# In every fourth slot, TensorE's update of W stands one pair of experts later

## The chip, the cores and the metric

The kernel runs on one core of one Trainium2 chip. The metric is the device time of one execution in microseconds (us), lower being better. Before the change three runs took 1006.75, 1006.24 and 1005.19 us; the median is 1006.24 us. PE is TensorE's matmul stream and PEld its weight loads, DVE is VectorE, ACT ScalarE, POOL GpSimd, SP the engine whose queue issues the DMAs.

## The reference, cut to what matters

The input x has 8 batches of 1024 time steps with 256 features, in float32. It is normalised (layer norm), and two things are computed from the result:

```python
xn = _layernorm(x, axis=-1)
# s: a linear layer learned online, one gradient step of W per time step
v = xn @ Wkv[d:].T + bkv[d:]
def step(W, inp):
    xt, vt = inp
    y = xt @ W.T
    gW = (2.0 / (b * d)) * ((y - vt).T @ xt)
    return (W - eta * gW, y)
# g: silu of a mixture of 16 linear experts, the gates being
#    the top 6 of a softmax over router logits, made to sum to one
out = sum over e of (xn @ expert_w[e]) * gate[:, e:e + 1]
x + s * silu(out)
```

## The kernel before, in words

**Tiles and slots.** The tokens go in 64 tiles of 128 rows: 16 time steps of all 8 batches. The main loop (lines 653 to 661) goes through the tiles i, and for each through eight pairs of experts. The stretch of the loop that belongs to tile i is called slot i here; a place in it is written (slot, pair) or as one number, 8 * slot + pair. At each place the function `experts` (line 530) does its pair: six matmuls (line 241) of 128x128 by 128x512 make `h`, one PSUM bank of 512 columns, 256 for each expert. There are three such banks (line 85), so a pair can only be started when the bank of the pair three places earlier has been read by both of its readers.

**Who reads h.** The even expert is multiplied by its gate and added to a running sum on DVE (`mix`, line 558). The odd one is multiplied by its gate on ACT (`part`, line 547) and added on POOL (line 550); this holds for experts 1 to 11. Experts 13 and 15 go to DVE like the even ones (line 47). So pair 3 is read by `mix_6` on DVE and `part_7` on ACT, and so on.

**The recurrence over W.** W^T lives in one PSUM bank, `wt_ps`. A tile goes through three steps, one after the other, and each needs the one before:

- `errors_1` (line 488): six matmuls of X with the current W (`pe`), then DVE and ACT make `p`, `p_hi`, `p_lo`.
- `errors_2` (line 505): three matmuls with the solved matrix U; then ACT makes `step_hi` (line 510) and DVE makes `step_lo` (line 512), and DVE also `hy` (line 516).
- `update` (line 518): six matmuls into `wt_ps`, of 128x128 by 128x256: hi by hi, lo by hi, hi by lo for each half of the features. The third and the sixth read `step_lo`. Then `new_state` (line 159) makes `wt_hi` on ACT (line 142) and `wt_lo` on DVE (line 143), which `errors_1` of the next tile reads.

**What sets the order.** TensorE and SP keep the order in which the code issues work (line 639). A table of events says what comes ahead of which pair. From tile 7 on, `errors_1`, `errors_2` and `update` of tile i come ahead of pairs 0, 3 and 5 of slot i; tiles 0 to 6 have places of their own (line 607), among them slot 6, where the update comes ahead of pair 7. The other engines are put in an order by a scheduler when the kernel is built; on the chip each engine then takes its instructions strictly in that order.

**Gates and U come by groups.** Gates, and the triangular solve for U, are made for four tiles at a time. The work of a group of tiles first to first + 3 lies ahead of it: each tile is projected five slots early, at pair 1 (`project_x`, line 583), and the last tile of a group also sets off `gates` (line 348), a row of about twenty small DVE operations. That happens in slots 6, 10, 14 and so on to 58. In the same slot DVE makes the first matrices of the solve (`q`, line 407), and TensorE does the first step of it, `q_ps` (`step_q`, line 395), ahead of pair 6. Because events at one place are done in the order in which they were put, and the recurrence is put first, an update at pair 6 would come ahead of `q_ps`.

Of the kernel before, what the change touches and what calls it, by code (L numbers as in the profile page):

```python
"""Layer norm, then an online-learned linear layer (one gradient step of W per time step) gated by
the silu of a top-6-of-16 mixture of linear experts, with a residual.

Tokens go in tiles of 128 rows: 16 time steps of all 8 batches, time-major. Within a tile the
recurrence is solved exactly: with A = c * X X^T restricted to strictly earlier time steps and
c = eta * 2 / (B * D), the errors of all steps are E = T (X W^T - V), T = (I + A)^-1, where W is the
weight before the tile, and W^T is then lowered by c * X^T E. The state W^T accumulates in one PSUM
bank.

U = T^T is built for a few tiles at a time from diagonal blocks of 32 rows, by Horner's rule  # L10
(I - C (I - C (I - C)), C = A^T), which merge into blocks of 64 and then 128 rows:
U_ab = -U_a C_ab U_b.

TensorE and the DMA queue keep the order given below; the other engines are scheduled around them.
All but the first tiles are transposed without TensorE: in blocks of 32 by VectorE, and the blocks
change places on their way through DRAM.

The large products split each float32 operand exactly into two float32r parts, x = hi + lo, and add
up hi*hi + hi*lo + lo*hi in float32; what is left out is below float32's own rounding.
"""  # L20

# [1 line left out]

# [11 lines left out]
PSUM = bass.MemoryType.PSUM  # L35
# [5 lines left out]
EPS = 1e-10  # L41
ABSENT = -3.0e38
TAKEN = 3.0e38
GROUP = 4
# [6 lines left out]
def ttt_moe_kernel(  # L51
# [13 lines left out]
    B, S, D = x.shape  # L65
# [10 lines left out]
    state = ctx.enter_context(tc.tile_pool(name="state", bufs=2))  # L76
# [3 lines left out]
    work = ctx.enter_context(tc.tile_pool(name="work", bufs=2))  # L80
# [10 lines left out]
    where = []  # L91
# [19 lines left out]
    def misc(name):  # L111
        return ps_misc.tile([P, 512], F32, tag="misc", name=name)

# [1 line left out]
    raws = {}  # L115

    def fetch_expert(e):
# [19 lines left out]
    make_identity(nc, ident)  # L137
    neg_half = const.tile([P, 1], F32)
    nc.gpsimd.memset(neg_half, -0.5)
    # transposed weights: W0^T the first state, [Wv^T | router^T] one moving operand  # L140
    def split(hi, lo, src, engine=None):
        nc.scalar.copy(hi, src)  # L142
        (engine or nc.vector).tensor_sub(lo, src, hi.bitcast(F32))  # L143
# [37 lines left out]
    def at(b, size=Q):  # L181
        return slice(b * size, (b + 1) * size)

# [1 line left out]
    class Prepared:  # L185
        pass

    tiles = {}

    def layernorm(i):  # L190
        q = tiles[i] = Prepared()
        xt = x_tile(i)
        st = small.tile([P, nc.vector.BN_STATS_DIM], F32, tag="st", name=f"st_{i}")
        nc.vector.bn_stats(st, xt)  # L194
        mv = small.tile([P, nc.vector.BN_AGGR_DIM], F32, tag="mv", name=f"mv_{i}")
        nc.vector.bn_aggr(mv, st)  # L196
        ve = small.tile([P, 1], F32, tag="ve", name=f"ve_{i}")
        nc.gpsimd.tensor_scalar_add(ve, mv[:, 1:2], LN_EPS)  # L198
        rstd = small.tile([P, 1], F32, tag="rstd", name=f"rstd_{i}")
        nc.gpsimd.tensor_tensor(rstd, ve, neg_half, ALU.pow)  # L200
        q.xn = work.tile([P, D], F32, tag="xn", name=f"xn_{i}", bufs=3)
        nc.vector.tensor_scalar(q.xn, xt, mv[:, 0:1], rstd, ALU.subtract, ALU.mult)  # L202
        if i < BY_PE:
            return
        q.xT = work.tile([P, KD * P], F32, tag="xT", name=f"xT_{i}", bufs=3)
        # blocks of 32 are transposed in place, and change places by way of DRAM
        xr = work.tile([P, D], F32, tag="xr", name=f"xr_{i}")
        nc.vector.transpose(
            xr.rearrange("p (c k t) -> p k c t", c=NQ, k=KD),
            q.xn.rearrange("p (k c t) -> p k c t", c=NQ, k=KD),  # L210
        )
        bounce = dram.tile([NQ, Q, NQ, KD * Q], F32, tag="bounce", name=f"bounce_{i}")
        nc.sync.dma_start(out=bounce.rearrange("b d c f -> (b d) (c f)"), in_=xr)
        for c in range(NQ):
            nc.sync.dma_start(
                out=q.xT[at(c), :].rearrange("p (b f) -> p b f", b=NQ),
                in_=bounce[:, :, c, :].rearrange("b d f -> d b f"),
            )
# [15 lines left out]
        split(q.xn_hi, q.xn_lo, q.xn, nc.gpsimd)  # L234

    def accumulate(o, hi, lo, rhs_hi, rhs_lo, first=True, **kw):
        # the terms with the moving low part come last: it is ready last
        terms = [t for a, b, r in zip(hi, lo, rhs_hi) for t in ((a, r), (b, r))]
        terms += zip(hi, rhs_lo)
        for m, (a, b) in enumerate(terms):  # L240
            nc.tensor.matmul(  # L241
                o, lhsT=a, rhs=b, start=first and m == 0, stop=(m == len(terms) - 1), **kw
            )

    def project(i, g, j):
        q = tiles[i]
        # X X^T = H H^T + H L^T + (H L^T)^T
        gram = misc(f"gram_{i}")
        for k in range(KD):
            nc.tensor.matmul(  # L250
                gram[:, : 2 * P], lhsT=q.xT_hi[:, k, :],
                rhs=q.xT_two[:, k, :, :].rearrange("p n t -> p (n t)"),
                start=(k == 0), stop=(k == KD - 1), skip_group_check=True,
            )
        q.gram, q.cross = gram, work.tile([P, P], F32R, tag="cross", name=f"cross_{i}")
        nc.scalar.copy(q.cross, gram[:, P : 2 * P])
        vr = misc(f"vr_{i}")
        accumulate(
            vr[:, :NVR],
            [q.xT_hi[:, k, :] for k in range(KD)], [q.xT_lo[:, k, :] for k in range(KD)],  # L260
            [w_vr[0][:, k, :] for k in range(KD)], [w_vr[1][:, k, :] for k in range(KD)],
        )
        nc.vector.tensor_add(g.lg[:, j, :NE], vr[:, D:NVR], bias[:, D:])  # L263
        q.vr = vr
# [11 lines left out]
        nc.vector.tensor_add(xx, q.gram[:, :P], q.cross.bitcast(F32))  # L276
        nc.vector.tensor_mul(g.a[:, j, :, :], xx.unsqueeze(1).broadcast_to([P, 2, P]), masks)

# [1 line left out]
    layernorm(0)  # L280
    transpose_w()
    ident_r = const.tile([P, P], F32R)
# [2 lines left out]
    for b in range(NQ):  # L285
# [3 lines left out]
    half_b = const.tile([P, D], F32)  # L289
    nc.scalar.mul(half_b, bias[:, :D], 0.5)  # L290

    # -c at strictly earlier time steps, in A's place and in A^T's
    ones = const.tile([P, P], F32)
    nc.gpsimd.memset(ones, 1.0)
    keep = const.tile([P, 2, P], F32)
    nc.gpsimd.affine_select(
        out=keep[:, 0, :], in_=ones, compare_op=ALU.is_ge, fill=0.0, base=-B,
# [3 lines left out]
        out=keep[:, 1, :], in_=ones, compare_op=ALU.is_gt, fill=0.0, base=0,  # L301
# [2 lines left out]
    masks = const.tile([P, 2, P], F32)  # L304
    nc.vector.tensor_scalar_mul(masks, keep, neg_c)

    # U and the first half of T by blocks: what is never written stays zero
    u_full, t_half = [], []
    for n in range(2):
        u = const.tile([P, GROUP, P], F32, tag=f"u_{n}", name=f"u_{n}")  # L310
# [8 lines left out]
    def open_group(n, first, count):  # L319
# [14 lines left out]
        for name, t in vars(stores[m]).items():  # L334
            if name in ("t", "z2"):
                setattr(g, name, t)
            else:
                setattr(g, name, t[:, j : j + count])
        # odd tiles keep the first half of T, and what comes of it, in the upper partitions
        g.halves = []  # L340
        for odd in range(2):
            js = [n for n in range(count) if (j + n) % 2 == odd]
# [5 lines left out]
    def gates(g):  # L348
# [5 lines left out]
        def narrow(name):  # L354
            return group.tile([P, GROUP], F32, tag=name, name=f"{name}_{n}", bufs=4)[:, :c]

        # the six largest logits, the first of equal ones, are marked; two absent values fill up to eight
        lg, top, d, ex = g.lg, wide("top", 8), wide("d"), wide("ex")
        marked, chosen, gate = wide("marked", NE + 2), wide("chosen"), wide("gate", bufs=4)
        for j in range(c):  # L360
# [12 lines left out]
            chosen, marked[:, :, :NE], TAKEN, ex, op0=ALU.is_equal, op1=ALU.mult  # L373
        )
        nc.vector.tensor_reduce(s_top, chosen, AX.X, ALU.add)
        # gates p / (sum p + EPS) with p = ex / s_all, then divided by max(their sum, EPS)
        nc.vector.scalar_tensor_tensor(den, s_all, EPS, s_top, op0=ALU.mult, op1=ALU.add)
        nc.vector.reciprocal(r_den, den)
        nc.vector.tensor_mul(total, s_top, r_den)
# [7 lines left out]
            q.u_hi, q.u_lo = g.u_hi[:, j, :], g.u_lo[:, j, :]  # L387

    def step_q(g, name, rhs, out):
        """I - C rhs for the diagonal blocks."""  # L390
        c = g.count
        ps = solving(f"{name}_ps_{g.n}")
        for j in range(c):
            for b in range(P // Q):
                nc.tensor.matmul(  # L395
                    ps[at(b), j * Q : (j + 1) * Q], lhsT=g.a[at(b), j, 0, at(b)],
                    rhs=rhs[at(b), j, :], start=True, stop=True, skip_group_check=True,
                )
        nc.vector.tensor_add(
            out, ps[:, : c * Q].rearrange("p (j q) -> p j q", q=Q),  # L400
            ident_q.unsqueeze(1).broadcast_to([P, c, Q]),
        )
# [58 lines left out]
    H = P // 2  # L461
# [22 lines left out]

    solve = [solve_1, solve_2, solve_3, solve_4, solve_5, solve_6]

# [1 line left out]
    def errors_1(i):  # L488
        q = tiles[i]
        q.pe = ps_rec.tile([P, 2 * D], F32, tag="pe", name=f"pe_{i}")  # L490
# [70 lines left out]
                q.mix[j] = new  # L561

    def finish(i):
        # x + y silu(m) = x + (y / 2) m (1 + tanh(m / 2))
        q = tiles[i]
        xt = x_tile(i)
        m = work.tile([P, D], F32, tag="m", name=f"m_{i}")
# [9 lines left out]
            out=out[:, i * TS : (i + 1) * TS, :].rearrange("b t d -> t b d"), in_=o  # L577
        )

# [1 line left out]
    opened = {}  # L581

    def project_x(i):
# [13 lines left out]
    def solve_x(n, m):  # L597
        solve[m](opened[n])

    # what comes before each (tile, pair of experts)  # L600
    events = {}

    def put(slot, pair, what, *args):
        events.setdefault((slot, pair), []).append((what, args))

    # the first tiles have a schedule of their own: (slot, pair) as 8 * slot + pair
    chain = {
        0: (3, 9, 10), 1: (13, 16, 18), 2: (21, 23, 25), 3: (27, 29, 31), 4: (33, 38, 40),
        5: (42, 45, 47), 6: (49, 51, 55),
    }  # L610
    for i in range(NT):
        spots = chain.get(i, (8 * i, 8 * i + 3, 8 * i + 5))
        for what, spot in zip((errors_1, errors_2, update), spots):
            if what is not update or i + 1 < NT:
                put(spot // 8, spot % 8, what, i)
        if i + 1 < NT:
            put(i + 1, 1, finish, i)
# [75 lines left out]
```

## Time and profile before

| What | Value |
|---|---|
| Median of three runs | 1006.24 us (1005.19 to 1006.75) |
| Profiled execution: span from first to last instruction | 1004.7 us |
| Matmuls of the experts (`h`), 3072 | 789.3 us, mean 402 ns each (they overlap) |
| Matmuls of the update (`wt_ps`), 126 of each of three kinds | 35.6, 35.6 and 37.0 us |
| Share of the span in which DVE, ACT, POOL are busy | 77%, 43%, 44% |
| Mean granted TensorE clock | 0.992 of full speed |

The profiled execution has only its span; what lies around the first and the last instruction is in the times of the three runs, which are 0.5 to 2.1 us above the span. In the groups of instructions a row names the line, the engine, the operation, what is written and read, and how often, then busy time, mean duration of one, and the idle time just ahead of them with what ended it. In a timeline a row has the start and the length in us, both from the span's start. A line such as L241 or L142 can be that of a helper that many steps call; the name of the tile then tells the steps apart. A matmul's row includes its filling and draining, so rows of matmuls overlap: what a matmul costs the stream is the distance from its start to the next start.

### The profile page before, as it was taken

To read this page: it belongs to the slowest core of one execution; us is meant where nothing else is said; L and a number is where in the kernel's file an instruction comes from. 1 tells how busy PE (TensorE), PEld (TensorE's weight loads), DVE (VectorE), ACT (ScalarE), POOL (GpSimd) and SP (SyncE) were. 2 spreads that over 40 slices of the span, in tenths; PEclk is the share of its full clock that TensorE was granted. 3 is DMA by queue.
4 is the path that set the end of the run, shared out by engine and by line. 5 is a ranking of instruction groups with operands and counts; after the bars stand their busy time and mean duration, and the time that the engine had idled before them with its cause. 6 is when DMAs were issued, how large, how long until landed. Compare 5 with 4: busy or idle time off the path is not lost.

```text
span 1004.7 us, 19617 instructions
## 1 busy us (share of the span) xinstructions
PE 977.6 (97%) x6672; PEld 799.9 (80%) x6672; DVE 770.0 (77%) x2225; ACT 436.5 (43%) x1174; POOL 440.8 (44%) x677
## 2 busy tenths in 40 slices
PE   5899999999999999999999999999999999999997
PEld 4677888878888887888878888887888878888785
DVE  7888797777878777787777878778787777867665
ACT  5454444344443534435344443534435344443432
POOL 6544344444344344444444344344444444344333
PEclk8899999999999999999999999999999999999999
DMA  7021111111111111111111111011111111100000
GB/s 231 17 53 49 39 27 43 37 27 43 39 27 42 28 37 43 38 27 44 38 28 43 38 28 43 24 42 43 36 29 43 38 28 43 35 25 11 12 11 11
DMA packets 67092, 38.65 MB, mean 38 GB/s; under 512 B 38176, under 2 KB 66992, under 8 KB 66992
## 3 DMA queue, kind: packets, MB, share of 16 engines
q1 hardware_dynamic: 66992, 37.41, 13.6%
q8 instruction: 52, 0.85, 0.3%
q14 instruction: 48, 0.39, 0.1%
HBM read 21.13 MB, written 16.25 MB: 37 GB/s over the span
## 4 chain that ended last, share of the span: by engine, by line
PE 77%; DVE 14%; issue 2%; POOL 2%; DMA 2%; ACT 2%; SPq 1%; POOLq 0%; DVEq 0%; ACTq 0%
PE h L241 59%; PE pe L241 6%; PE wt_ps L241 4%; PE vr L241 3%; DVE q L407 3%; DVE mix L558 2%; DMA x<-in_L_attn_x_dram 1%; PE gram L250 1%; DVE marked L366 1%; POOL mix L550 1%; DVE st L194 1%; ACT part L547 1%; DVE o L574 1%; DVE d L362 1%; PE uq_ps L395 1%
## 5 line engine op out<-in xcount | busy, mean ns | idle before, releaser
L241 PE MATMUL h<-we,xT_two 128*128 128x512 f32 x3072 | 789.3, 402 | 4.5 <-DVE mix L558 2.5
L241 PEld LDWEIGHTS h<-we,xT_two 128*128 128x128 f32 x3072 | 554.5, 189 | 120.1 <-issue 2.7
L558 DVE SCALAR_TENSOR_TENSOR mix<-h,gate,mix 128x256 f32<-128x256 f32 x576 | 265.6, 475 | 112.0 <-PE h L241 80.1
L547 ACT ACTIVATE part<-h,gate 128x256 f32<-128x256 f32 x384 | 182.1, 474 | 293.1 <-DVE mix L558 171.4
L550 POOL TENSOR_TENSOR mix<-mix,part 128x256 f32<-128x256 f32 x256 | 188.7, 737 | 131.4 <-ACT part L547 124.0
L572 POOL TENSOR_TENSOR my<-m,hy 128x256 f32<-128x256 f32 x64 | 47.3, 739 | 159.0 <-DVE m L568 159.0
L550 POOL TENSOR_TENSOR mix<-part,part 128x256 f32<-128x256 f32 x64 | 47.9, 749 | 72.3 <-ACT part L547 72.3
L575 POOL TENSOR_TENSOR o<-o,x 128x256 f32<-128x256 f32 x63 | 46.5, 738 | 69.4 <-DVE lg L263 59.2
L194 DVE BATCH_NORM_STATS2 st<-x 128x6 f32<-128x256 f32 x64 | 27.1, 425 | 49.9 <-DMA x<-in_L_attn_x_dram 49.5
L241 PE MATMUL vr<-w_vr,xT_two 128*128 128x272 f32 x384 | 59.2, 290 | 0.0
L202 DVE TENSOR_SCALAR xn<-x,mv,rstd 128x256 f32<-128x256 f32 x64 | 49.0, 765 | 12.2 <-POOL rstd L200 11.9
L143 DVE TENSOR_TENSOR wt_lo<-wt_ps,wt_hi 128x512 fp32r<-128x512 f32 x64 | 42.9, 671 | 19.6 <-ACT wt_hi L142 19.5
L142 ACT CAST xT_two<-xT 128x256 fp32r<-128x256 f32 x60 | 24.4, 407 | 71.9 <-PE h L241 69.9
L198 POOL TENSOR_SCALAR ve<-mv 128x1 f32<-128x1 f32 x64 | 14.5, 228 | 91.2 <-DVE mv L196 56.4
L143 POOL TENSOR_TENSOR xn_lo<-xn,xn_hi 128x256 fp32r<-128x256 f32 x64 | 47.7, 746 | 14.2 <-ACT xn_hi L142 13.9
L142 ACT CAST p_hi<-p 128x256 fp32r<-128x256 f32 x64 | 26.0, 406 | 63.6 <-DVE p L498 63.5
L241 PEld LDWEIGHTS vr<-w_vr,xT_two 128*128 128x128 f32 x384 | 52.4, 191 | 0.0
L510 ACT ACTIVATE step_hi<-pe,neg_c 128x256 fp32r<-128x256 f32 x64 | 30.4, 474 | 50.5 <-PE pe L241 50.2
L241 PEld LDWEIGHTS pe<-wt_hi,xT_two 128*128 128x128 f32 x256 | 39.2, 189 | 5.9
L142 ACT CAST wt_hi<-wt_ps 128x512 fp32r<-128x512 f32 x64 | 37.2, 581 | 10.8 <-PE wt_ps L241 10.3
L241 PE MATMUL pe<-wt_hi,xT_two 128*128 128x256 f32 x256 | 40.7, 281 | 0.0
L143 DVE TENSOR_TENSOR p_lo<-p,p_hi 128x256 fp32r<-128x256 f32 x64 | 39.2, 612 | 0.9 <-ACT p_hi L142 0.4
(115 smaller groups left out, 1186.7 us busy)
## 6 DMA issues: line engine op xcount, KB each, us to landing
x<-in_L_attn_x_dram SPq DMA_DIRECT2D x64, 128.0 KB, 2.7
out_dram<-o SPq DMA_DIRECT2D x64, 128.0 KB, 2.3
bounce<-xr SPq DMA_DIRECT2D x60, 128.0 KB, 2.4
xT<-bounce SPq DMA_DIRECT2D x240, 32.0 KB, 1.8
raw<-in_L_ffn_expert_w_dram SPq DMA_DIRECT2D x16, 256.0 KB, 5.0
w_raw<-in_L_attn_Wkv_dram SPq DMA_DIRECT2D x1, 256.0 KB, 3.1
w_raw<-in_L_attn_W_dram SPq DMA_DIRECT2D x1, 256.0 KB, 5.2
bias<-in_L_attn_bkv_dram SPq DMA_DIRECT2D x1, 128.0 KB, 4.5
```

The lines of the kernel that those rows point to most:

```text
L142: nc.scalar.copy(hi, src)
L143: (engine or nc.vector).tensor_sub(lo, src, hi.bitcast(F32))
L194: nc.vector.bn_stats(st, xt)
L202: nc.vector.tensor_scalar(q.xn, xt, mv[:, 0:1], rstd, ALU.subtract, ALU.mult)
L241: nc.tensor.matmul(o, lhsT=a, rhs=b, start=first and m == 0, stop=(m == len(terms) - 1), **kw)
L407: nc.vector.tensor_add(g.q1[at(b)], g.a[at(b), :, 1, at(b)], ident_q[at(b), :].unsqueeze(1).broadcast_to([Q, c, Q]),)
L510: nc.scalar.mul(q.step_hi, e, neg_c)
L547: nc.scalar.mul(part, he, gate)
L550: nc.gpsimd.tensor_add(new, q.mix[1], part)
L558: nc.vector.scalar_tensor_tensor(new, he, gate, q.mix[j], op0=ALU.mult, op1=ALU.add)
L572: nc.gpsimd.tensor_mul(my, m, q.hy)
L575: (nc.vector if i == NT - 1 else nc.gpsimd).tensor_add(o, o, xt)
```

## The change

The update of a tile whose number is 2 more than a multiple of four is put ahead of pair 6 in place of pair 5. It holds for tiles 10, 14, ..., 62, which makes 14 updates; tiles 0 to 6 keep their own places. Comments and the text at the head of the file are also gone, which changes no instruction. No instruction is added or removed.

```diff
     for i in range(NT):
-        spots = chain.get(i, (8 * i, 8 * i + 3, 8 * i + 5))
+
+        late = 1 if i % GROUP == GROUP - 2 else 0
+        spots = chain.get(i, (8 * i, 8 * i + 3, 8 * i + 5 + late))
         for what, spot in zip((errors_1, errors_2, update), spots):
             if what is not update or i + 1 < NT:
                 put(spot // 8, spot % 8, what, i)
```

On TensorE the order around the change goes from h_4, wt_ps, h_5, q_ps, h_6, h_7 to h_4, h_5, wt_ps, q_ps, h_6, h_7. The scheduler of the other engines answers to it. In slots 10 to 54 DVE's row xn, wt_lo, xr, mix_10, q, mix_12 becomes xn, mix_10, xr, q, wt_lo, mix_12. ACT's row part_7, wt_hi, xn_hi, part_9, part_11 becomes part_7, part_9, wt_hi, xn_hi, part_11. POOL adds mix_9 ahead of making xn_lo, where it had been behind. In slots 58 and 62, where no further tile is normalised, wt_lo moves behind mix_10 (in slot 58 behind q too) and wt_hi behind part_11. The order of the DMAs on SP stays as it is.

## The prediction

> **What bounds the kernel now.** I read the page first: busy shares, then the chain that ended last.
>
> ```profile
> span 1004.7 us, 19617 instructions
> PE 977.6 (97%) x6672; PEld 799.9 (80%) x6672; DVE 770.0 (77%) x2225; ACT 436.5 (43%) x1174; POOL 440.8 (44%) x677
> PE 77%; DVE 14%; issue 2%; POOL 2%; DMA 2%; ACT 2%; SPq 1%; POOLq 0%; DVEq 0%; ACTq 0%
> ```
>
> TensorE is nearly always at work, and 77% of the chain is its own. The 14% of DVE say that in some stretches DVE, not TensorE, ends last. Which ones, the list of waits tells; of all waits of TensorE's weight loads on the recurrence, this is the largest:
>
> ```profile
> PEld wt_ps L241 <- DVE step_lo L512: 5.2, 12, 0.6
> ```
>
> Twelve waits, 5.2 us together, the longest 0.6. I looked up each in TensorE's timeline: they are the updates of slots 10, 14, ..., 54, one each. Slot 26 stands for all:
>
> ```profile
> 442.32 0.28 PE L241 MATMUL wt_ps<-step_hi,xn_hi 128*128 128x256 f32 x1
> 442.44 0.28 PE L241 MATMUL wt_ps<-step_hi,xn_lo 128*128 128x256 f32 x1
> 443.08 0.39 PE L241 MATMUL wt_ps<-step_lo,xn_hi 128*128 128x256 f32 x1 [0.37 <-DVE step_lo L512]
> 443.31 0.28 PE L241 MATMUL wt_ps<-step_hi,xn_hi 128*128 128x256 f32 x1
> ...
> 443.66 1.57 PE L241 MATMUL h<-we,xT_two 128*128 128x512 f32 x6
> 445.16 0.45 PE L395 MATMUL q_ps<-q,a 32*32 32x32 f32 x32
> 445.55 3.06 PE L241 MATMUL h<-we,xT_two 128*128 128x512 f32 x12
> ```
>
> Starts should be 0.12 us apart; between the second and the third there are 0.64. What DVE does then:
>
> ```profile
> 441.09 1.09 DVE L407 TENSOR_TENSOR q<-a,ident_q 32x128 f32<-32x128 f32 x2
> 442.22 0.43 DVE L194 BATCH_NORM_STATS2 st<-x 128x6 f32<-128x256 f32 x1
> 442.56 0.47 DVE L512 SCALAR_TENSOR_TENSOR step_lo<-pe,neg_c,step_hi 128x256 fp32r<-128x256 f32 x1
> ...
> 443.36 0.45 DVE L558 SCALAR_TENSOR_TENSOR mix<-h,gate,mix 128x256 f32<-128x256 f32 x1
> ```
>
> No idle time stands in these rows: DVE has worked without a named wait since 433.3 through gates and first solve matrices, and step_lo comes in its turn. Its input was ready at 440.2 (step_hi on ACT, 439.71 and 0.47). In slot 58, the last with gates, no tile is left to normalise, and the same six matmuls run undisturbed.
>
> **What the wait costs.** From the first wt_ps to the next h it takes 0.71 us undisturbed (slot 6, 144.56 to 145.27; slot 58, 925.37 to 926.08). In the twelve slots it takes 1.19, 1.20, 1.10, 1.13, 1.34, 1.19, 1.22, 1.07, 1.41, 1.08, 1.29 and 1.17, in sum 14.39. The excess is 14.39 - 12 x 0.71 = 5.87 us, 0.49 a slot. That it reaches the end follows from the distances between updates: slot 10 to 14 is 60.36 us (201.04 to 261.40), slot 26 to 30 is 60.51, slot 42 to 46 is 60.57. Less the excess of the first slot (0.48, 0.63, 0.70) each is 59.87 or 59.88. TensorE never makes up what it lost, and loses nothing else that varies.
>
> **The change part by part.** Call t = 0 the start of the first wt_ps before. Steps, all on TensorE: a pair of experts takes 1.41 (18 matmuls from 428.90 to 433.12 are three pairs), the update 0.71, q_ps 0.48 (443.66 to 445.55 is a pair and q_ps). Afterwards h_5 starts at 0, wt_ps at 1.41, q_ps at 2.12, h_6 at 2.60, h_7 at 4.01, the next tile's pe at 5.41.
>
> - step_lo: let in the third matmul at 0.50 to 0.83 (0.76 in slot 26). It is wanted at 1.41 + 0.24 = 1.65. The wait goes in all twelve slots, with 0.8 to spare: -5.87.
> - h_5 goes early, into the bank of h_2. Its last reader, part_5, ran 440.39 to 440.86, 1.4 ahead. Nothing.
> - h_6 goes into the bank of h_3, whose last reader is part_7: 443.91 plus 0.47, so t = 2.06 (slot 42, the worst, 2.12). Neither mix_6 nor part_7 changes place. h_6 is wanted at 2.60: 0.48 or more to spare. Nothing, but this is the closest.
> - wt_hi: ACT now does part_9 first, to 2.06 + 0.49 = 2.55, then wt_hi in 0.58, to 3.13. Wanted at 5.41. Nothing.
> - wt_lo: DVE reaches xn at 444.90 (0.81), ending at 3.39. Then come mix_10 0.44, xr 0.43, q 0.27 and wt_lo 0.68, at most to 5.21. q needs q_ps, done near 2.7. The first pe matmul with wt_lo is at 5.41 + 0.47 = 5.88. It has 0.67 to spare where it had 2.6. Nothing.
> - xn_hi and xn_lo of a later tile overwrite the updated tile's: they stood behind wt_hi before and still do. POOL does mix_9 first, so mix_11 still ends near 5.2, ahead of its old 6.2. Nothing. No DMA is moved.
> - Slots 58 and 62 had no wait: a swap of equal pieces. Nothing.
>
> One neighbourhood is new: q_ps right behind wt_ps. uq_ps right behind pe, matmuls of the same shape, costs 0.47 (448.45 to 449.63, less 0.71); behind h it is 0.48. The whole block cannot cost less than the 0.39 from its first start to the next h. So 13 times between -0.09 and +0.02, -1.2 to +0.3 us; I take 0, the nearest row.
>
> Sum: 1004.7 - 5.9 = 998.8 us of span. The median lies 1.5 above the profiled span; the same distance gives 1006.24 - 5.87 = **1000.4 us**.
>
> **A rule weighed.** part_7 began 0.10 after mix_6 ended (443.81), although ACT had stood idle for 3.05 us and the two read different halves of the bank; so the bank comes free only after both, one behind the other. The Trainium skill, PSUM — Partial Sum Buffer, section on bank collisions, says why: two engines must not touch one bank at a time, reads included, so a dependency is put between them. That speaks against the change, which sends h_5 and h_6 to their banks sooner. Without it part_7 could end about 0.55 earlier and h_6 would have 1.0 to spare; with it 0.5. The sum is the same either way, and the next rival gets more chance.
>
> **The rivals.**
>
> - *The bank of h_3 takes the wait over.* Slot 6 shows it: there pairs 3, 4 and 5 ran back to back, with no update between, and then:
>
> ```profile
> 141.86 0.45 PE L395 MATMUL q_ps<-q,a 32*32 32x32 f32 x32
> 143.05 1.67 PE L241 MATMUL h<-we,xT_two 128*128 128x512 f32 x6 [0.74 <-ACT part L547]
> ```
>
>  h_6 could start 5.49 after h_3 (137.56). With the update ahead of it, it is wanted 5.41 after h_3. Slot 6's lateness would cost 0.08 a slot, 1.0 us: 1001.4. If part_7 slips to cost 0.25 a slot, 3.0 us come back: 1003.4. Against it: in the twelve slots part_7 is 0.57 earlier against h_3 than in slot 6 (4.87 to 5.44).
> - *DVE is the bound and the wait only moves.* The chain runs without TensorE from y_ps at 405.19 over a store, a load and DVE to step_lo at 443.08. If that stretched with the time won, nothing would be gained: 1006.2. Against it: it starts from TensorE again each group, and DVE idles elsewhere, 1.21 us ahead of st in slot 25 and 0.78 ahead of mix_13.
> - *wt_lo comes too late, slower than before.* It now stands behind q, which waits for TensorE, and ahead of mix_12 and mix_13. If DVE met ahead of it what it meets a little later, 0.78 of waiting for POOL and three mixes in 1.27, wt_lo would be 2.05 late. pe would stand 2.05 - 0.67 = 1.38 a slot in place of 0.49: 12 x 0.89 = 10.7 more, 1016.9. It loses from 1.16 of lateness on, and measurably from 1.33. Against it: in slot 6 wt_ps is only 2.10 ahead of pe, wt_lo ran 146.26 to 146.94, and pe took it at 147.13 without a wait.
>
> **How the numbers follow.** Forecast 0.79, bank of h_3 0.08, wait only moved 0.06, wt_lo late 0.07. The forecast's own range is -1.2 to +0.3 from the new neighbourhood, with about 0.3 of scatter at the ends: 999.0 to 1001.0. To be safe for 8 in 10 it is stretched over most of the first rival, to 1002.9. A measurement of this kernel can tell about 0.2% (2 us) from no change. Faster by more: 0.79 + 0.08 = 0.87. Within: 0.06. Slower: 0.07.
>
> **What will show it.** Right: the row of waits of wt_ps on step_lo is gone, each slot has 0.71 from the first wt_ps to the next start, updates of slots 10 to 54 are 59.87 apart, and DVE drops from the chain. Bank rival: idle time of h_6 ended by ACT part. Bound rival: the same 5 to 6 us under another name. Slow rival: pe waiting for DVE wt_lo. I would be wrong above all if DVE's rows ahead of step_lo came later against h_4 than now, though nothing ahead of them is moved.

## The result, and the profile after

The changed kernel took 1001.03 us (median of 6 runs, 999.11 to 1002.76) against 1006.79 us for the kernel before, measured beside it (median of 6 runs, 1005.19 to 1008.68). The ratio is 0.9937, with a 95% interval of 0.9923 to 0.9951: 0.5 to 0.8% faster.

The page of the changed kernel, first its span, then the shares of the chain that ended last:

```profile
span 1000.1 us, 19603 instructions
PE 92%; DVE 4%; issue 1%; DMA 1%; POOL 1%; ACT 0%; SPq 0%; POOLq 0%; ACTq 0%
```

TensorE's share of the chain has gone from 77% to 92%, DVE's from 14% to 4%. In the list of waits of TensorE's weight loads there is no row any more in which wt_ps waits for step_lo. Slot 26 again, TensorE's timeline (start, length, what):

```profile
443.28 0.28 PE L241 MATMUL wt_ps<-step_hi,xn_hi 128*128 128x256 f32 x1
443.40 0.28 PE L241 MATMUL wt_ps<-step_hi,xn_lo 128*128 128x256 f32 x1
443.51 0.28 PE L241 MATMUL wt_ps<-step_lo,xn_hi 128*128 128x256 f32 x1
443.63 0.28 PE L241 MATMUL wt_ps<-step_hi,xn_hi 128*128 128x256 f32 x1
...
444.08 0.45 PE L395 MATMUL q_ps<-q,a 32*32 32x32 f32 x32
444.47 3.06 PE L241 MATMUL h<-we,xT_two 128*128 128x512 f32 x12
447.37 0.64 PE L241 MATMUL pe<-wt_hi,xT_two 128*128 128x256 f32 x4
447.84 0.40 PE L241 MATMUL pe<-wt_lo,xT_two 128*128 128x256 f32 x2
```

The matmuls of the update start 0.12 apart, and pe takes wt_lo without a gap. DVE and ACT in the same slot of the changed kernel:

```profile
442.35 0.47 DVE L512 SCALAR_TENSOR_TENSOR step_lo<-pe,neg_c,step_hi 128x256 fp32r<-128x256 f32 x1
...
443.14 0.46 DVE L558 SCALAR_TENSOR_TENSOR mix<-h,gate,mix 128x256 f32<-128x256 f32 x1
...
446.35 0.67 DVE L143 TENSOR_TENSOR wt_lo<-wt_ps,wt_hi 128x512 fp32r<-128x512 f32 x1
```

```profile
443.69 1.01 ACT L547 ACTIVATE part<-h,gate 128x256 f32<-128x256 f32 x2 [3.05 <-DVE total L379]
```

DVE did not become faster. In this slot step_lo ended 0.71 us after the end of pair 4 before (443.03 and 442.32), and ends 0.95 after it now (442.82 and 441.87). But TensorE now asks for it 1.64 after the end of pair 4.

**One measure for all runs.** The two spans differ by only 4.6 us (1004.7 and 1000.1, where 998.8 was forecast), although more was won. (An execution's time lies about 2 us above its own span; the profiled one here took 1002.19.) The reason lies ahead of tile 7, where the two kernels issue the same work in the same order: the first matmul of errors_1 of tile 7 started at 146.66 before and at 148.03 after. So I use D, the distance from the first matmul of errors_1 of tile 7 to that of tile 63, which leaves this stretch out. Each kernel has one trace, so each D below is of one execution. D was 839.08 before and is 833.20 after: 5.88 less. The updates of slots 10, 14, ..., 58 now are 59.85 to 59.88 apart, against 60.23 to 60.57.

### The profile page after: what moved, and what is told of

Read it like the earlier page. It is cut to its first block, busy times and chain, and to the rows that moved or that the text cites. A ratio compares the mean times of both kernels' runs of the same rounds, so it can differ in the third digit from the quotient of the medians.

```text
span 1000.1 us, 19603 instructions
## 1 busy us (share of the span) xinstructions
PE 972.9 (97%) x6672; PEld 799.4 (80%) x6672; DVE 768.3 (77%) x2225; ACT 437.3 (44%) x1174; POOL 440.9 (44%) x677
## 4 chain that ended last, share of the span: by engine, by line
PE 92%; DVE 4%; issue 1%; DMA 1%; POOL 1%; ACT 0%; SPq 0%; POOLq 0%; ACTq 0%
PE h L241 70%; PE pe L241 6%; PE vr L241 5%; PE wt_ps L241 4%; PE gram L250 2%; DVE q L407 1%; PE gram L268 1%; PE z_ps L466 1%; PE y_ps L451 1%; PE uq_ps L395 1%; PE y_ps L477 1%; PE q_ps L395 1%; PE z_ps L433 1%; DVE mix L558 0%; DMA eta_sb<-in_L_attn_eta_dram 0%
```

## The experiments

All kernels were run in rounds beside the kernel before. "Changed kernel" is the one with the update at pair 6. The first four share the runs of before that their ratios are taken against, and so do five to eight and nine to eleven. Rows of waits are those from 150 us on, so that the first tiles are left out.

**One: half of the slots.**

```diff
-        late = 1 if i % GROUP == GROUP - 2 else 0
+        late = 1 if i % (2 * GROUP) == GROUP - 2 else 0
```

> The update is put one pair later in every eighth slot only (10, 18, 26, 34, 42, 50, 58). Measure: D, the distance from the first matmul of errors_1 of tile 7 to that of tile 63; 839.1 us before, 833.2 after the full change. Theory (the gain is the sum of single waits of TensorE on step_lo, each worth its own slot): slots 10, 18, 26, 34, 42 and 50 had lost 0.48, 0.39, 0.63, 0.51, 0.70 and 0.58, in sum 3.3, so D is 835.8 and the other six waits stay as they are. Rival (the win is in something shared, such as DVE catching up over several groups): D is not in between, either near 839 or near 833.

Measured: D 836.47; ratio 0.9951 (0.9936 to 0.9966). The six updates left at pair 5 lost 0.62, 0.43, 0.42, 0.41, 0.55 and 0.41, in sum 2.84, and the six moved ones nothing. A seventh wait of 0.47 stood in slot 23, which has no gates. 833.20 + 2.84 + 0.47 = 836.51. So each wait is worth its own slot, and the rival of a shared gain falls. What happened in slot 23 is seen in DVE's timeline, in the kernel before:

```profile
397.29 0.43 DVE L194 BATCH_NORM_STATS2 st<-x 128x6 f32<-128x256 f32 x1 [2.68 <-DMA x<-in_L_attn_x_dram]
```

In this run:

```profile
392.74 0.43 DVE L277 TENSOR_TENSOR a<-xx,masks 128x256 f32<-128x256 f32 x1
396.67 0.43 DVE L194 BATCH_NORM_STATS2 st<-x 128x6 f32<-128x256 f32 x1 [3.50 <-DMA x<-in_L_attn_x_dram]
```

One load of x came late: it landed 4.2 us after it was issued, where the same load took 3.4 before and the median of all loads before was 2.7. DVE stood 3.50 us in its row at `st`, where it stood 2.68 at the same place before, and step_lo was behind it.

**Two: the same move in other slots.**

```diff
-        late = 1 if i % GROUP == GROUP - 2 else 0
+        late = 1 if i % GROUP == 0 else 0
```

> The update is put one pair later in slots 8, 12, ..., 60, in which no gates come, and stands at pair 5 in slots 10, 14, ..., 62. Theory (only the wait on step_lo behind the gates is worth anything): D stays 839.1 within 0.5, all twelve waits of about 0.5 us stay, and the later update costs nothing. Rival (the later place of the update helps as such, by the order of pieces on TensorE or of ACT and POOL): D falls by some us here too.

Measured: D 839.54; ratio 0.9996 (0.9984 to 1.0008). The waits of this run have the old row, with all twelve:

```profile
PEld wt_ps L241 <- DVE step_lo L512: 5.7, 12, 0.8
```

The later place is worth nothing by itself, neither way. The twelve waits were larger in this execution than in the trace of before, 6.39 us of excess in place of 5.87, which accounts for the 0.46 by which D is longer. So what the change wins depends by about half a microsecond on the execution.

**Three: two pairs later.**

```diff
-        late = 1 if i % GROUP == GROUP - 2 else 0
+        late = 2 if i % GROUP == GROUP - 2 else 0
```

> In slots 10, 14, ..., 62 the update is put two pairs later, ahead of pair 7, so that q_ps and pair 6 come ahead of it. Theory: the wait on step_lo is gone (-5.9), but pair 6 is now wanted 1.89 us after the end of pair 4, and the bank of h_3 comes free 1.85 to 2.2 after it, so part_7 makes TensorE wait 0 to 0.3 a slot, 1.1 in all; wt_lo, now behind mix_13, comes about 0.3 late for pe, 3.6 in all. D is 838, between 834.4 and 840. Rival (as in slot 6, where pair 6 stood 0.79): the bank alone costs 9.5 and D is 842.7 or more.

Measured: D 839.74; ratio 0.9994 (0.9983 to 1.0006). The wait on step_lo is gone, and all of the gain with it. The rows of waits that stand in its place (total us, times, longest):

```profile
PEld pe L241 <- DVE wt_lo L143: 3.2, 12, 0.3
PEld h L241 <- ACT part L547: 2.8, 9, 0.5
```

Both were expected, but only one in its size: wt_lo is at 3.2 for 3.6, the bank of h_3 at 2.8 for 1.1. In slot 26 h_6 started at 444.82 where 444.49 was possible, and the first pe with wt_lo at 449.12 where 448.91 was. With the update in between, as in the change, the bank has time to come free; without it, it has not. The bank's stand of 0.79 in slot 6 is not reached.

**Four: the cause taken away instead.** The four additions that make q, ahead of step_lo on DVE, go to POOL from tile 8 on; the update is at pair 5 as before.

```diff
-            nc.vector.tensor_add(
+            (nc.gpsimd if g.n > 3 else nc.vector).tensor_add(
                 g.q1[at(b)], g.a[at(b), :, 1, at(b)],
```

> The update stays at pair 5 as before; instead the four additions that make the first solve matrices q, which stand right ahead of step_lo on DVE (1.75 us a group of four tiles), are done by POOL in the groups from tile 8 on. Theory (DVE's queue ahead of step_lo is the cause of the wait): step_lo comes some 1.7 us earlier, all twelve waits go without the update being moved, and D is 833.2 within 0.6. Rival (the change helped by moving the update or by the new order on ACT and POOL): the waits may go, but something else makes TensorE stand and D stays above 836; or POOL's additions come too late for q_ps and TensorE stands there.

Measured: D 835.97; ratio 0.9952 (0.9936 to 0.9969). All twelve updates take 0.71 from the first wt_ps to the next h, though the update has not moved: step_lo starts on the average 0.77 before the end of pair 4, where it had started 0.10 after it. So it was DVE's row that kept step_lo back. But D is 2.8 above the changed kernel's, not within 0.6. New waits stand in other slots of this run:

```profile
PEld gram L268 <- ACT cross L256: 1.6, 3, 0.6
...
PEld gram L250 <- DVE xT_two L143: 1.1, 4, 0.5
...
PEld wt_ps L241 <- DVE step_lo L512: 0.3, 1, 0.3
```

They are at four of the twelve distances between updates above all (60.64, 60.20, 60.45, 60.51), the rest being 59.88 to 59.95. So what the rival named comes about, if just under its 836: the waits go, and something else makes TensorE stand. The traces show what. gram is the product of X with itself for a later tile; its second part (line 268) reads `cross`, which ACT makes. In slot 43, which lost 0.57:

```profile
691.80 0.27 ACT L256 CAST cross<-gram 128x128 fp32r<-128x128 f32 x1
...
692.12 0.33 PE L268 MATMUL gram<-ident_r,cross 128*128 128x128 f32 x1 [0.51 <-ACT cross L256]
```

cross ended here 6.08 after the first matmul of errors_1, and gram started 0.05 behind it; undisturbed it starts at 5.56. In slot 47, which lost nothing, cross ended at 5.43. The lateness can be followed back: against errors_1, POOL's rstd, DVE's xn and xT_two and ACT's cross are all 0.62 to 0.65 later in slot 43 than in slot 47. POOL had stood 0.94 for a `part` from ACT at the sum (line 550) just ahead of that rstd, and 0.14 just ahead of the other. Waits of gram for a late cross, in slots 15, 35, 43, 51 and 55, make 1.7 of the 2.8; the rest stands in slots 7, 11, 13 and 14, at other waits.

**Five to seven: the cover measured.** step_lo is computed more than once, with the same result, in slots 10, 14, ..., 62; `n` is 2 in the order of before, then 2 and 3 in the changed kernel.

```diff
+        for _ in range(n if i >= 7 and i % GROUP == GROUP - 2 else 1):
             nc.vector.scalar_tensor_tensor(
                 q.step_lo, e, neg_c, q.step_hi.bitcast(F32), op0=ALU.mult, op1=ALU.subtract
             )
```

> The order of TensorE is that of before; step_lo is computed twice, with the same result, in slots 10, 14, ..., 62, which lets DVE finish it about 0.97 us later (r_den 0.09, mix_6 0.39, mv 0.09 and the second step_lo 0.40 come between). Theory (TensorE stands from the moment at which it wants step_lo until DVE has it): each wait grows from 0.49 to about 1.35, 16.2 us in all twelve slots, and D, from errors_1 of tile 7 to that of tile 63, is 849.4 against 839.1. Rival (the wait is only one of several that end close together): D grows by less than half of that, under 845.

Measured: D 850.93; ratio 1.0125 (1.0099 to 1.0152). From the first wt_ps to the next h the twelve updates take 25.42 in all, so they lose 25.42 - 8.52 = 16.90 for 16.2 expected. Slot 58, which I had left out, loses 0.85 as well.

```profile
PEld wt_ps L241 <- DVE step_lo L513: 17.0, 13, 1.7
```

> The changed kernel with the same doubled step_lo. Theory (the change gave step_lo 1.41 us more, of which 0.8 is left over on the worst slot): step_lo now ends at 1.47 to 1.80 after the end of pair 4 and is wanted at 1.65, so nearly nothing is lost: 0.3 in all, D 833.5 against 833.2. Rival (the cover is thin and another wait takes over at once, the bank of h_3 or wt_lo): D rises by 3 us or more.

Measured: D 834.33; ratio 0.9946 (0.9921 to 0.9972). The same delay that cost 11.9 in the order of before costs 1.1 here, 1.0 of it at four updates (slots 14, 26, 30 and 50: 0.14, 0.39, 0.22 and 0.29). That is 0.8 more than expected, because step_lo scatters more than I had allowed for, see below.

> The changed kernel with step_lo computed three times in those slots: total, mix_8 and a third step_lo come on top, 0.90 us. Theory: step_lo ends 0.84 after it is wanted on the average, all twelve waits are back, 10.1 us in all, D 843.3. Rival (the slack of step_lo is larger than worked out, or the later DVE work eats more): D below 838, or above 847 with pe waiting for wt_lo as well.

Measured: D 843.89; ratio 1.0050 (1.0034 to 1.0066).

```profile
PEld wt_ps L241 <- DVE step_lo L513: 9.8, 13, 1.2
```

The old row is back, 13 times (slot 58 is in it), and no other new one; pe does not wait for wt_lo. The theory holds to 0.6 us.

**Eight: the changed kernel again**, with no edit.

> The changed kernel once more, for a second trace. Theory (what the change does lies behind tile 7 and the stretch ahead of it, in which both kernels are the same, scatters by itself): D is 833.2 within 0.5, and the time of the first 7 tiles, 146.7 before and 148.0 after in the first two traces, differs again by about 1 us either way. Rival (the changed kernel starts later): the first 7 tiles take 148 again, and more than in the traces of the kernels that start like before.

Measured: D 833.38; ratio 0.9943 (0.9923 to 0.9962); median 999.59 against 1006.47, 6.88 less. Nearly all of the 0.18 more in D stands in slot 14, where gram waited for xT_two. errors_1 of tile 7 started at 145.05, 3 us sooner than in the first trace of the same kernel. In the other runs of this study it started between 144.97 and 148.72, in no order with the edit. The rival falls.

**Nine and ten: the nearest other limit.** In the changed kernel mix_6 is computed n = 2 or 3 times, with the same result, in the same slots. That puts part_7 off, and so the bank of h_3, but not step_lo.

```diff
                 else:
+                    for _ in range(n if e == 6 and i >= 7 and i % GROUP == GROUP - 2 else 1):
                         nc.vector.scalar_tensor_tensor(
                             new, he, gate, q.mix[j], op0=ALU.mult, op1=ALU.add
                         )
```

> The changed kernel, mix_6 computed twice with the same result in slots 10, 14, ..., 62. step_lo stays as early as it is; only part_7, the last reader of the bank of h_3, is put off, by about 0.5 us (mv, total and the second mix_6 come between), to 2.7 after the end of pair 4, while h_6 wants the bank at 2.60. Theory (part_7 has 0.4 to 0.5 to spare and no more): TensorE stands 0.13 a slot ahead of h_6, 1.6 us in all, and D, from errors_1 of tile 7 to that of tile 63, is 834.9 against 833.3. Rival (the bank is wanted sooner than worked out): the whole 0.5 is lost, D 839. Other rival (much more to spare): D stays 833.3.

Measured: D 834.04, ratio 0.9933 (0.9917 to 0.9950).

> The same with mix_6 computed three times: part_7 ends about 3.3 after the end of pair 4. Theory: TensorE stands 0.72 a slot ahead of h_6, ended by ACT part, 8.6 us in all, D 842; pe does not wait for wt_lo, since the standing gives wt_lo its time back. Rival (wt_lo, 1.0 later as well, is the nearer limit): the standing is ahead of pe, ended by DVE wt_lo.

Measured: D 840.73, ratio 0.9998 (0.9985 to 1.0010). This run's wait, twelve times:

```profile
PEld h L241 <- ACT part L547: 6.9, 12, 0.9
```

part_7 ended on the average 1.97 after the end of pair 4 in the changed kernel, and ends 2.54 and 3.07 after it here. So 0.57 of delay is nearly free, with 0.8 us more in D, and 1.10 costs 7.5 us and eats the whole gain. For a later mix_6 the bank of h_3 is the next limit, about 0.57 away on the average, and wt_lo is farther: no row has pe waiting for it.

**Eleven: late everywhere.**

```diff
-        late = 1 if i % GROUP == GROUP - 2 else 0
+        late = 1
```

> The update is put one pair later in every slot from 7 on, not only where gates come. Theory (in the other slots step_lo is in time, and 2.9 us from the update to pe are enough for wt_hi and wt_lo): D is 833.3 as with the change, neither better nor worse by more than 0.5. Rival (in slots without gates something leans on the earlier update, such as wt_lo or the bank): D rises by 2 us or more. A version that beats the change would show as D under 833.

Measured: median 1000.58, ratio 0.9927 (0.9906 to 0.9948), which this measurement cannot tell from the change. D is 836.76 in its one trace, 3.6 above the change, so the rival's 2 us are passed. Ten of the twelve distances between updates are 59.86 to 59.88; the two others are 62.22 and 61.03. In both of those stretches loads of x came late, the second time so:

```profile
636.82 0.43 DVE L194 BATCH_NORM_STATS2 st<-x 128x6 f32<-128x256 f32 x1 [3.85 <-DMA x<-in_L_attn_x_dram]
```

Of the loads behind this, the one in slot 39 was issued 5.64 after errors_1 began, no later than in the changed kernel (5.68), and took 4.9 us to land where it took 3.6 there. So it was the transfer that was slow. Whether the later update has a part in that, one trace cannot say. But it has thinned the cover: in slot 39 TensorE stood 0.89 for a `part` ahead of pair 5, and the update, which takes 0.71, would have come there in the changed kernel. It is no better than the change in any case, so no faster version was found.

## Why the prediction was right

Forecast were 1000.4 us and 5.87 us won. Measured were 1001.03 us, a difference of 5.76 between the medians, and 5.88 in D. That 5.88 and 5.87 lie so close is in part luck: the second trace of the changed kernel gives 5.70, its medians 6.88, and the same twelve waits made 6.39 in the second experiment.

- **The wait and its price.** Right. The twelve excesses, 5.87, are what D lost. That they add up slot by slot is shown by the first experiment, that the place alone does nothing by the second, and that DVE's row is the cause by the fourth to seventh.
- **"TensorE never makes up what it lost, and loses nothing else that varies."** Right for slots 10 to 54: without waits the distance is 59.87. It holds on the whole only where loads are in time; the first and eleventh runs show losses from late ones, and the second trace of the changed kernel one distance of 60.04.
- **step_lo has 0.8 to spare.** The mean is right, the worst is too kind. I carried DVE's times over from before as if they were fixed against TensorE. In twelve slots step_lo started, on the average, 0.10 after the end of pair 4 before, 0.16 after and 0.12 in the second trace; but the latest start went from 0.31 to 0.48 and 0.50. That leaves 0.6 on the worst slot, and explains why the doubled step_lo cost 1.1 and not 0.3.
- **h_6 has 0.48 or more to spare.** The same: part_7 ended at up to 2.29 and 2.32 for 2.12, so 0.25 to 0.3 on the worst slot. Among the limits that the forecast names it still was the closest, and the ninth and tenth experiments found it there.
- **A path that the forecast leaves out.** The second part of gram wants cross. Before, cross ended at most 5.21 after errors_1 began, in slots 11, 15, ..., 55; in the two traces of the changed kernel it ended at up to 5.38 and 5.40. The fourth experiment shows gram start 0.05 behind a late cross, and gram is wanted at 5.56. So only about 0.1 was left on the worst slot, less than for the bank of h_3. That this path cost nothing was not worked out, and so was luck.
- **wt_lo ends at most at 5.21 and is wanted at 5.88.** Right: it ended at 4.6 to 5.2. pe itself came at 5.50 in slot 26 and not at 5.41, since two pairs behind q_ps take 2.90 and not 2.82; both orders have this.
- **The new neighbourhood of wt_ps and q_ps costs nothing.** Right in sum: from the first wt_ps to the first h behind q_ps it is 1.19 in slot 26 (443.28 to 444.47), which is 0.71 and 0.48. The sign that was named, 0.71 from the first wt_ps to the next start, did not show: q_ps started at 0.80, and h 0.39 behind it. Before, uq_ps behind pe had the same split (448.45, 449.25, 449.63).
- **The rivals.** The bank did not take over, the wait did not move, wt_lo was not late. All three exist: the bank and wt_lo appear as soon as the update goes one pair further (third experiment).
- **Other engines on one bank.** In the changed kernel too ACT stood idle for 3.05 us and began part_7 at 443.69, right behind mix_6 (443.14 to 443.60). The row names total, but that ended at 443.73, when part_7 had begun. This agrees with the rule of the Trainium skill, PSUM — Partial Sum Buffer, section on bank collisions, that two engines reading one bank are kept apart; no run here let them read it together. The ninth and tenth experiments show its price: what puts off mix_6 puts off part_7, by 0.57 and 1.10, and TensorE with it.

## What to carry to other kernels

An engine that keeps its order stands at the first instruction whose operand is late, even if it has other work that is ready, as TensorE stood about 0.5 us in each of twelve slots with h_5 ready. Swapping the two pieces wins the wait, if the list of waits shows it again and again at one place, and the piece that goes ahead is ready and lasts longer than the wait (1.41 here). Then work out, for each thing that is moved, how long ahead of its use it is ready, and see what is next late: here one pair later won 5.9 us, two pairs won nothing. Take the worst slot and not the average, and do not take one engine's times as fixed against another's when the order changes: the latest start of step_lo moved by 0.2. To learn how thick such a cover is, compute the late operand twice and three times and look where the time begins to rise.

## What the runs showed that was not expected

The stretch ahead of tile 7 took 144.97 to 148.72 us in the thirteen traces, a range of 3.75, which is more than half of the change's worth; two spans are therefore no measure of an edit that acts later, and a distance inside the trace is. Single loads of x came late, so that DVE stood 3.50 or 3.85 us at `st` where it stood 2.68 and 2.72 at the same places before, and what stands behind `st` in DVE's row then makes TensorE stand in slots that have cover otherwise. They are not spread evenly: from tile 14 on, the loads of tiles 19 and 47 took over 3.3 us from issue to landing in ten of the thirteen traces each, against a median of 2.7 to 2.8 for all. Why these two, no run here shows.
